# Three key heads computed in the recurrence's prologue, and a new order for the attention's first tiles

## The chip, the cores and the metric

The kernel runs on one core of a Trainium2 chip. The metric is the device time of one execution in microseconds (us), taken as the median of the runs. The core has five engines, each with a queue of its own that it works off in order: TensorE (PE in the profile, PEld for its weight loads), VectorE (DVE), ScalarE (ACT), GpSimd (POOL) and SyncE (SP), which here issues most of the DMAs.

## What is computed

The reference is a network of four parts with residual connections, on x of 4 batches x 512 rows x 512 columns and a context ctx of 4 x 512 x 256:

```python
x = x + _L0_xattn_ref(ctx_1024, _layernorm(x), ...)   # a state-space recurrence over the rows
x = x + _L0_ffn_ref(_layernorm(x), ...)               # 64 experts, 8 for each row
x = x + _L1_xattn_ref(_layernorm(x), ctx_1024, ...)   # attention, 16 heads of 128
x = x + _L1_ffn_ref(_layernorm(x), w1, w2)            # feed-forward, quantized weights and inputs
```

Two of them matter here. The recurrence, for each of 512 channels (four blocks of 128, c) and 16 states n, walks over the 512 rows:

```python
state = state * exp(delta * A) + (delta * u) * B      # delta, u, B, C come from projections of ctx
y = sum over n of state * C                           # then + D * u, times silu of the normed x
```

The attention's keys depend on ctx alone, and not on x:

```python
k = (ctx @ Wk).reshape(B, Skv, H, D)
k = k * rsqrt(mean(k * k, axis=-1) + 1e-5) * gk
```

So the 64 key heads (4 batches x 16) can be computed at any time before the attention reads them.

## The kernel before

The kernel is one program in four stages, each of which writes down the order of its instructions by hand: every call in the source puts its instructions at the end of its engines' queues, in the order of the calls.

**The recurrence** (`ssm_phase`) runs over `seq`, 128 steps q = (batch b, channel block c, pair of states i), 32 steps to a batch. A step needs three things. `inputs(q)` (L494) multiplies `du` by the rows of B, on POOL, into `dBu` (128x1024). `decays(q)` (L505) makes exp(delta * A) on ACT into `dA`. `scan(q)` runs a scan on DVE (L519) and multiplies by the rows of C (L520), on POOL where i is 0, 2 or 4 and on DVE otherwise. TensorE turns and sums the results (`sums`, L525). Beside this the steps carry work for the next batch (`ahead`), the values of the attention (`values`, L476, one PSUM bank with the tag pv, and `take_values`, L482, on ACT), and keys.

Ahead of the loop stands a prologue for batch 0: projections (`conv_0`), a convolution, `project`, `dt` (L420), then on ACT `steps_a` and `steps_ln`, on DVE `steps_b` (L445 to L447), which ends with delta, on POOL `step_du` (L455, and L458, which writes a reset into delta's first column after it was read), on ACT `decays(0)` and `decays(1)`, on POOL `inputs(0)` and `inputs(1)`. `rows(b, g)` (L413) loads four rows of B (`bb`) and four of C (`cb`), 1 MB each, spread over all partitions; for batch 0 the first group is queued after `take_project`, then `load_wv(0)` (L469) and the other three groups. At q = 0 ACT gets `silu_gz(0)` (L393), with a table load before and after it; at q = 1 TensorE gets a transposition of its result and then the first `values`; at q = 2 ACT gets `take_values` ahead of `decays(3)`.

**A key head** (`Keys`) is four calls. `task` (L1216) multiplies the context by the head's part of Wk, two blocks of 128 deep, into a PSUM bank `pk`. `evict` squares it (L1225) and scales it (L1226) on ACT, and stores kT by a DMA on SP (L1227). `squares` (L1236) sums the squares by eight small matmuls with a column of ones into `kpss`. `take` (L1248) copies the mean squares on ACT and stores them (L1250). `row` and `psum` say where the two rows and two banks are taken from.

Of the 64 heads, 15 stand in batches 0 to 2 of the recurrence (for the next batch), 16 in its last batch (those of batch 0, one every second step, `plan_key` from `last_q` on, their weights loaded four heads at a time by `key_at(..., keys.load, ...)` into two buffers with the tag dA), 17 in the routing stage, and 16, listed in `KEYS_LATE`, at the start of the attention.

**Routing and experts** follow. In the experts' stage the mean squares of all heads but the late ones are turned into factors (`key_norms`) and stored as rows.

**The attention** (`attend`) begins with the four row tiles of batch 0, i = 0 to 3. Their order is made from a list of `later(time, call)`, sorted by time; the times are only an order. Eight late keys come first (`some_keys`). Then 32 gathers of experts' results on POOL (`fetch`, L1874), each followed by an addition on DVE (`add`, L1882); after every eighth a tile is complete, gets its statistics (`stats`, L1888 on DVE and L1892, L1894 on POOL) and is normed (`normed`, xn_c, L1900). Tile i starts at `at = FRONT + i * WINDOW`: `turn_x` (L1907) turns the tile, `queries` for head groups 0 and 1 (L1953), `norm_q` (L1956 on ACT, L1962 on DVE, then rq by L1964, L1965 on POOL), `scale_q` (qn, L1971 on DVE), `turn_q` (pqt, L1980), `scores` (psc, L1987, then mx on DVE L1990 and e on ACT L1993), `weights` (L1998, L1999), `turn` (pet, L2052). Two late keys stand in each tile: `key_task` and `key_ends` (`squares`, then `take`). `last_norms` and `last_keys` then make the late heads' factors. After the tiles a loop over heads and tiles does the rest; the last stage, the feed-forward part, is woven into it.

Of the kernel before, what the change touches and what calls it, by code (L numbers as in the profile page):

```python
# [17 lines left out]
F32 = mybir.dt.float32  # L18
# [7 lines left out]
ALU = mybir.AluOpType  # L26
# [4 lines left out]
P = 128  # L31
B, S, DM = 4, 512, 512
NT = B * S // P
NC = DM // P
# [24 lines left out]
H, HD = 16, 128  # L59
HG = 4  # L60

KEYS_LATE = [(b, h) for b in (2, 3) for h in range(8, H)]
DH = 2048
RESET = 1e30
MAGIC = 12582912.0
# [177 lines left out]
def ssm_phase(ctx, cm, x_all, w, kv, router_stats):  # L243
# [4 lines left out]
    tc, nc = cm.tc, cm.nc  # L248
# [4 lines left out]
    ps = ctx.enter_context(tc.tile_pool(name="a_ps", bufs=1, space=PSUM))  # L253
    py = ctx.enter_context(tc.tile_pool(name="a_py", bufs=1, space=PSUM))
    pda = ctx.enter_context(tc.tile_pool(name="a_pda", bufs=2, space=PSUM))
    KC = CTX // P
# [10 lines left out]
    def load_ctx(b, again=False):  # L267

        t = pool[2].tile([P, KC, S], F32, name="ctxb")
        nc.sync.dma_start(t, w["ctxT"][:, b * S:(b + 1) * S].rearrange("(k p) s -> p k s", p=P))  # L270
        if again:
            st[b]["ctx"] = t
            return
        st[b] = dict(ctx=t, u=[], gz=[], delta=[], du=[], bb=[], cb=[],
                     mv=small.tile([P, NC, 2], F32, name="mv"))
# [3 lines left out]
    load_ctx(0)  # L279
    load_x(0)  # L280
    load_ctx(1)
    vecs = {}
    for n, shape in (("conv_w", [P, NC, DC]), ("conv_b", [P, NC]), ("D", [P, NC])):
        t = vecs[n] = cp.tile(shape, F32, name=f"v_{n}")
# [104 lines left out]
    def silu_gz(b):  # L389
        s = st[b]  # L390
        for c in range(NC):
            gz = pool[4].tile([P, S], F32, name="gz")
            nc.scalar.activation(gz, x_all[:, b * NC + c, :], AF.Silu, bias=s["nmr"][:, c:c + 1],  # L393
                                 scale=s["rstd"][:, c:c + 1])
            s["gz"].append(gz)
        tables(nc)
# [12 lines left out]
    def rows(b, g):  # L409

        for name, row in (("bb", g * NG), ("cb", DS + g * NG)):
            t = pool[4].tile([P, NG, S], F32, name=name, tag=name)
            nc.sync.dma_start(  # L413
                t, bc_dram[b, row:row + NG, :].unsqueeze(0).to_broadcast([P, NG, S]))
            st[b][name].append(t)

    def dt(b, c):

        pdt = st[b]["pdt"] = ps.tile([P, S], F32, name="pdt", tag="pa")
        nc.tensor.matmul(pdt, dtT[:, c * P:(c + 1) * P], st[b]["xd"][0:DR + 1, :], start=True,  # L420
                         stop=True)

    def steps_a(b):

        s = st[b]
        pdt = s["pdt"]
        s["e"] = pool[1].tile([P, S], F32, name="e")
        s["relu"] = pool[2].tile([P, S], F32, name="delta")
        nc.scalar.activation(s["e"], pdt, AF.Abs)
        nc.scalar.activation(s["relu"], pdt, AF.Relu)  # L430
        nc.scalar.activation(s["e"], s["e"], AF.Exp, scale=-1.0)
# [8 lines left out]
    def steps_b(b):  # L440


        s = st[b]
        t, delta = s.pop("pdt"), s.pop("relu")
        nc.vector.scalar_tensor_tensor(t, t, 1.0, s["e"], ALU.subtract, ALU.subtract)  # L445
        nc.vector.tensor_tensor(t, s["ln"], t, ALU.subtract)
        nc.vector.tensor_tensor(delta, delta, t, ALU.add)  # L447
        s["delta"].append(delta)

    def step_du(b):  # L450
        s = st[b]
        c = len(s["du"])
        delta = s["delta"][c]
        du = pool[2].tile([P, S], F32, name="du")
        nc.gpsimd.tensor_tensor(du, delta, s["u"][c], ALU.mult)  # L455


        nc.gpsimd.memset(delta[:, 0:1], RESET)  # L458
        s["du"].append(du)


# [24 lines left out]
    seq = [(b, c, i) for b in range(B) for c in range(NC) for i in range(NP)]  # L486
    dBus, dAs, hcs, yTs = {}, {}, {}, {}

    def inputs(q):
        if q < len(seq):  # L490
            b, c, i = seq[q]
            j = i % 2 * 2
            dBus[q] = pool[3].tile([P, 2, S], F32, name="dBu")
            nc.gpsimd.tensor_tensor(dBus[q], st[b]["bb"][i // 2][:, j:j + 2, :],  # L494
                                    st[b]["du"][c].unsqueeze(1).to_broadcast([P, 2, S]), ALU.mult)

    def decays(q, early=False):

        if q < len(seq) and q not in dAs:
            b, c, i = seq[q]  # L500
            dAs[q] = (pool[2].tile([P, 2, S], F32, name="dA") if early else
                      pda.tile([P, 2, S], F32, name="dA"))
            for j in range(2):
                n = 2 * i + j
                nc.scalar.activation(dAs[q][:, j, :], st[b]["delta"][c], AF.Exp,  # L505
                                     scale=negA[:, c, n:n + 1])
# [108 lines left out]
    def plan_key(q, b, h, bank):  # L615
        key_at(q, True, key_task, b, h, bank)
        key_at(q + 2, False, keys.evict)
        key_at(q + 2, True, keys.squares)
        key_at(q + 3, False, keys.take)
# [3 lines left out]
            key_at(b * SL + s - 3, False, keys.load, j, j + 1, pool[2], "k_w")  # L623
            plan_key(b * SL + s, b + 1, j, bank)
    last_q = (B - 1) * SL
    for h in range(H):
        plan_key(last_q + 2 * h, 0, h, "pin")
    for h, q in ((0, last_q - 8), (HG, last_q + 6), (2 * HG, last_q + 8), (3 * HG, last_q + 16)):
        key_at(q, True, keys.load, h, h + HG, pool[2], "dA")

    def key_steps(q, ends):
# [18 lines left out]
        stats(0, c)  # L650
    norm(0)
    dt(0, 0)
    steps_a(0)
    steps_ln(0)
    steps_b(0)
    step_du(0)
    decays(0)
    decays(1)
    inputs(0)
    inputs(1)  # L660
    load_wv(0)
    for g in range(1, DS // NG):
        rows(0, g)
    for q, (b, c, i) in enumerate(seq):
        inputs(q + 2)

        ahead_of = b + 1 < B and q % 2 == 0 and q > 0
        if ahead_of:
            take_values(*last)
        decays(q + 1)  # L670
        key_steps(q, False)
        if b > 0 and q % SL == 1:
            rows(b, DS // NG - 1)
        if i == 2 and q > 2:
            result(*seq[q - 3][:2])
        scan(q)
        if i == 1:
            direct(b, c)
        if q == 0:
            silu_gz(0)  # L680
        if q % SL == 8 and b + 1 < B:
            load_x(b + 1)
        if i == 2:
            take_gate(b, c)

        to = seq[q // NP * NP + NP][0:2] if q + NP < len(seq) else None
        if to is not None:
            if i == 3:
                steps_a(to[0])
                steps_ln(to[0])  # L690
            if i == 5:
                step_du(to[0])
        if b + 1 < B:
            ahead(b + 1, q % SL)
        if i == 1:
            gate(b, c)
        if q % 8 == 2 and q + 8 < len(seq):
            load_wv(q // 2 + 4)
        if q % 2:
            values((b + 1) % B, q % SL // 2, wvs[q // 8])  # L700
        elif q > 0 and not ahead_of:
            take_values(*last)
        last = (b + 1) % B, q % SL // 2
        sums(q - 1)
        if to is not None:
            if i == 2:
                dt(*to)
            if i == 4:
                steps_b(to[0])
        if b + 1 < B:  # L710
            ahead_ends(b + 1, q % SL)
        key_steps(q, True)
# [1130 lines left out]
def attend(ctx, cm, x_all, w, kv, y_dram, wk, pos, tern, late, ctx_k, wk_k, out):  # L1843
# [422 lines left out]
    keys = Keys(cm, w, kv, small, key_row, key_bank,  # L2266
                lambda b: (ctx_k[b], 0), direct=ms)
    keys.wk = wk_k
    first = KEYS_LATE[0][1]

    steps = []

    def later(time, f, *a):
        steps.append((time, len(steps), f, a))

    START, GAP, FLIGHT = 3.0, 1.35, 6.0
    FRONT, WINDOW = 21.0, 14.5

    wide = [pool[1].tile([P, KB, S], F32, name="yg_first", tag="eT")]
    wide += [pool[2].tile([P, HG, DM], F32, name="yg_more", tag="Wo") for _ in range(2)]  # L2280
# [27 lines left out]
    for i in range(NC):  # L2308
        end = START + ((i + 1) * TOPK - 1) * GAP + FLIGHT
        later(end + 0.1, stats, i, "c")  # L2310
        later(end + 2.3, normed, i, "c")
        at = FRONT + i * WINDOW
        later(at, turn_x, i)
        later(at + 0.5, key_task)
        later(at + 2.2, queries, 0, 0, i)
        later(at + 5.6, key_ends)
        later(at + 6.4, norm_q, 0, 0)
        later(at + 6.5, queries, 0, 1, i)
        later(at + 8.5, scale_q, 0, 0)
        later(at + 10, turn_q, 0, 0, i)  # L2320
        later(at + 10.4, key_task)
        later(at + 10.8, norm_q, 0, 1)
        later(at + 12.1, scores, 0, i)
        later(at + 12.9, scale_q, 0, 1)
        later(at + 13, key_ends)
        later(at + 14, turn_q, 0, 1, i)
        if i < KB - 1:
            later(at + 14.7, weights, 0, i)
        if i < KB - 2:
            later(at + 15, turn, 0, i)  # L2330
# [9 lines left out]
    def last_keys():  # L2340
        pr = ptr.tile([n_ms, P], F32, name="pkr", tag="pt")
        nc.tensor.transpose(pr, ms, cm.ident)
        rows = pool[1].tile([n_ms, P], F32, name="k_rows", tag="xn_d")
        nc.scalar.copy(rows, pr)
        for b in (2, 3):
            at = (b * H + first) * KB
            nc.sync.dma_start(kv["r"][at:at + n_ms // 2, :],
                              rows[(b - 2) * n_ms // 2:(b - 1) * n_ms // 2, :])


    for *_, f, a in sorted(steps, key=lambda x: x[:2]):
# [192 lines left out]
```

## Time and profile before

| | us |
|---|---|
| median of 3 runs | 2475.75 (2473.74 to 2478.19) |
| the profiled execution | 2472.46 |
| its span, first to last instruction | 2470.7 |
| TensorE busy in the span | 2337.7 (95%) |
| DVE, ACT, POOL busy | 1595.2, 1386.1, 1344.1 |
| first scan of the recurrence starts | 34.57 |
| last dBu of the recurrence starts (POOL) | 503.58 |
| first late key of the attention starts (TensorE) | 1310.51 |
| last pqt of the first four tiles starts (TensorE) | 1404.86 |

The profile is of one execution. A line of the timeline gives the start and the duration in us, the engine, the source line, the operation, the output and inputs by their names, the shapes, the number of instructions merged into the line, and in brackets the engine's idle time before it with what ended it. The page's busy rows cut the span into 40 equal slices; a digit is the busy share in tenths. A line of the waits names who waited for whom, then the total in us, the number of waits and the longest. The granted TensorE clock is given as a share of full speed.

### The profile page before, as it was taken

Reading aid. Unit: us, or ns where it says so; the run is one execution under the profiler, and the core shown is the slowest. Engines: PE = TensorE matmul, PEld = TensorE weight load, DVE = VectorE, ACT = ScalarE, POOL = GpSimd, SP = SyncE. Lnnn points to the kernel's source line nnn. Section 1 sums busy time; section 2 is a strip of 40 time slices with the busy share of each in tenths; the row PEclk is TensorE's granted clock in tenths of the full one; section 3 lists DMA queues with packets and bytes.
Section 4 is the critical chain, followed back from the end, with each engine's and each line's share of the span. In section 5 each row is a group of like instructions: output and inputs, shape, how many; then the busy total and the mean of one; then the engine's idle time right before and its main releaser. Section 6 shows DMA issues by size and latency. Waiting matters only on the chain. (4 is left out here: it accounts for less than half of the span.)

```text
span 2470.7 us, 29274 instructions
## 1 busy us (share of the span) xinstructions
PE 2337.7 (95%) x8915; PEld 1275.5 (52%) x8915; DVE 1595.2 (65%) x2848; ACT 1386.1 (56%) x2599; POOL 1344.1 (54%) x1323
## 2 busy tenths in 40 slices
PE   6989998988899999999998999999999999999998
PEld 2555555655556666666674444444444444444443
DVE  6999998966343444444324577667776777666655
ACT  6777777755333333342323466666666767667654
POOL 7999999950344455444434356356544665333323
PEclk8999999998999999999998999999999999999999
DMA  5252626343677777989866568778866887666530
GB/s 212 90 210 95 219 85 232 112 151 119 194 233 227 229 243 236 314 308 336 302 210 211 163 179 217 163 181 187 207 159 149 200 202 173 138 156 147 136 75 24
DMA packets 454245, 458.69 MB, mean 186 GB/s; under 512 B 289239, under 2 KB 330279, under 8 KB 449984
## 3 DMA queue, kind: packets, MB, share of 16 engines
q1 hardware_dynamic: 410622, 299.80, 43.4%
q0 software_dynamic: 41408, 156.76, 19.8%
q8 instruction: 73, 1.20, 0.2%
q14 instruction: 92, 0.75, 0.1%
q10 hardware_dynamic: 2050, 0.18, 0.1%
HBM read 312.74 MB, written 79.82 MB: 159 GB/s over the span
## 5 line engine op out<-in xcount | busy, mean ns | idle before, releaser
L1336 PE MATMUL pg<-xT,wg 128*128 128x284 f32 (+12 forms) x1536 | 392.7, 399 | 2.0 <-ACT xT L1303 1.1
L1990 DVE TENSOR_REDUCE mx<-psc 128x1 f32<-128x512 f32 x256 | 176.1, 688 | 244.4 <-PE psc L1987 244.0
L2018 POOL COPY planes<-e 128x512 int16<-128x512 int16 x174 | 119.1, 684 | 392.3 <-DVE e L1999 230.7
L1336 PEld LDWEIGHTS pg<-xT,wg 128*128 128x128 f32 x1536 | 277.8, 191 | 91.6 <-issue 40.9
L494 POOL TENSOR_TENSOR dBu<-bb,du 128x1024 f32<-128x1024 f32 x128 | 304.3, 2398 | 2.7 <-DVE dA L519 1.8
L1993 ACT ACTIVATE e<-psc,mx 128x512 f32<-128x512 f32 x256 | 176.3, 688 | 149.6 <-DVE mx L1990 81.8
L1987 PE MATMUL psc<-kT,qT 128*128 128x512 f32 x512 | 260.0, 594 | 0.0
L2059 PE MATMUL po<-eT,v 128*128 128x512 f32 x512 | 236.8, 605 | 10.4 <-ACT eT L2053 8.6
L1257 POOL DMA_INDIRECT xg<-xn_dram,tok x168 | 177.5, 1056 | 116.5 <-PE pt L1300 51.4
L1953 PE MATMUL pq<-Wq,xnT 128*128 128x512 f32 x512 | 232.7, 597 | 4.3 <-ACT xnT L1909 3.9
L2068 PE MATMUL px<-Wo,oT 128*128 128x512 f32 x512 | 231.2, 595 | 0.4 <-DVE qn L1971 0.4
L505 ACT ACTIVATE dA<-delta,negA 128x512 f32<-128x512 f32 x256 | 176.5, 695 | 52.1 <-DVE hc L520 29.1
L519 DVE TENSOR_TENSOR_SCAN dA<-dA,dBu 128x1024 f32<-128x1024 f32 x80 | 185.4, 2318 | 14.6 <-ACT dA L505 4.9
L1257 POOL DMA_INDIRECT wd<-down,widx x64 | 63.1, 986 | 237.9 <-PE po L1370 222.3
L2059 PEld LDWEIGHTS po<-eT,v 128*128 128x128 f32 x512 | 92.0, 189 | 147.5 <-issue 91.8
L1381 ACT COPY yo<-po 128x512 f32<-128x512 f32 (+3 forms) x64 | 37.5, 586 | 224.7 <-PE po L1370 185.3
L1953 PEld LDWEIGHTS pq<-Wq,xnT 128*128 128x128 f32 x512 | 96.5, 191 | 129.7 <-issue 110.4
L525 PEld LDWEIGHTS yT<-ident,hc 128*128 128x128 f32 x1024 | 119.5, 144 | 77.3 <-issue 40.5
L2068 PEld LDWEIGHTS px<-Wo,oT 128*128 128x128 f32 x512 | 95.1, 190 | 123.3 <-issue 102.8
L1874 POOL DMA_INDIRECT yg<-y_dram,pos x108 | 119.8, 1109 | 62.7 <-issue 50.4
L525 PE MATMUL yT<-ident,hc 128*128 128x128 f32 x1024 | 133.2, 278 | 19.8 <-DVE yg L559 9.2
L1381 DVE COPY yo<-po 128x512 f32<-128x512 f32 x68 | 46.9, 691 | 159.4 <-PE po L1370 159.4
(378 smaller groups left out, 4686.2 us busy)
## 6 DMA issues: line engine op xcount, KB each, us to landing
y_dram<-yo SPq DMA_DIRECT2D x110, 256.0 KB
bb<-bc_dram SPq DMA_DIRECT2D x16, 1024.0 KB
cb<-bc_dram SPq DMA_DIRECT2D x16, 1024.0 KB
v_dram<-v SPq DMA_DIRECT2D x64, 256.0 KB
k_dram<-k_kT SPq DMA_DIRECT2D x64, 256.0 KB
kT<-k_dram SPq DMA_DIRECT2D x64, 256.0 KB
rk<-r_dram SPq DMA_DIRECT2D x64, 256.0 KB
v<-v_dram SPq DMA_DIRECT2D x64, 256.0 KB
```

The source lines that it names most:

```text
L494: nc.gpsimd.tensor_tensor(dBus[q], st[b]["bb"][i // 2][:, j:j + 2, :], st[b]["du"][c].unsqueeze(1).to_broadcast([P, 2, S]), ALU.mult)
L505: nc.scalar.activation(dAs[q][:, j, :], st[b]["delta"][c], AF.Exp, scale=negA[:, c, n:n + 1])
L519: nc.vector.tensor_tensor_scan(*flat, 0.0, ALU.mult, ALU.add)
L525: nc.tensor.matmul(yT[:, lc, :], t[:, lc * P:(lc + 1) * P], cm.ident, is_transpose=True, start=first and lc == 0, stop=last, skip_group_ch ...
L1257: nc.gpsimd.indirect_dma_start(out=t[0:n, :], out_offset=None, in_=table, in_offset=bass.IndirectOffsetOnAxis(ap=index, axis=0))
L1336: nc.tensor.matmul(pg[:, 0:n], s["wg"][:, c, m * P:(m + 1) * P], s["xT"][:, c, 0:n], start=c == 0, stop=c == NC - 1)
L1953: nc.tensor.matmul(pq.rearrange("p h d -> p (h d)"), xnTs[b * NC + i][:, c, :], s["Wq"][:, c, :], start=c == 0, stop=c == NC - 1)
L1987: nc.tensor.matmul(pscore, st[b, g]["qT"][:, h, i * P:(i + 1) * P], ks[n], start=True, stop=True)
L1990: nc.vector.tensor_reduce(mx, pscore, AX.X, ALU.max, negate=True)
L1993: nc.scalar.activation(e, pscore, AF.Exp, bias=mx, accum_out=tot)
L2059: nc.tensor.matmul(po, v[:, kc, :], eT[:, kc, :], start=kc == 0, stop=kc == KB - 1)
L2068: nc.tensor.matmul(px, oTs[j * HG + h][:, i * P:(i + 1) * P], st[b, g]["Wo"][:, h, :], start=h == 0, stop=h == HG - 1)
```

## The change

Three heads of batch 0 (h = 0 to 2) move into the prologue. Their weights get a DMA of their own on SP, after the first loads, in a buffer of the tag Wv. Their two rows are parts of `x_all` that are not loaded yet (row tiles 15 down to 10), their banks are pin, yT and pin for `pk`, and pv for all three `kpss`. Two tasks are queued on TensorE after `dt`; the evictions and takes are queued on ACT after `steps_ln` and between the decays; the last take after `silu_gz(0)`. `load_wv(0)` and the row loads are called earlier, in the same order among themselves.

`step_du(0)` and `inputs(0)` of the first step go from POOL to DVE.

In the last batch of the recurrence the 16 places for keys are kept. The 13 other heads of batch 0 come first, then heads 13 to 15 of batch 3, which were late ones; the weight loads for heads 4 on come 6 steps earlier. `KEYS_LATE` shrinks from 16 to 13: in the attention's first tiles, tile 0 keeps two keys, and tiles 1 to 3 have one each. `WINDOW` goes from 14.5 to 12.0, which also puts the next tile's `turn_x` and first `key_task` ahead of `scores` and of the second `turn_q`; and the second `key_ends` goes from 13 to 12.2.

```diff
+EARLY = 3
-KEYS_LATE = [(b, h) for b in (2, 3) for h in range(8, H)]
+KEYS_LATE = [(b, h) for b in (2, 3) for h in range(8, H - EARLY * (b == 3))]
...
     load_ctx(1)
+    wk_first = pool[2].tile([P, KC, EARLY * HD], F32, name="k_w", tag="Wv",
+                            padded_shape=[P, KC, HG * HD])
+    nc.sync.dma_start(wk_first, w["Wk"][:, 0:EARLY * HD].rearrange("(k p) e -> p k e", p=P))
...
-    def step_du(b):
+    def step_du(b, by=nc.gpsimd):
...
-        nc.gpsimd.tensor_tensor(du, delta, s["u"][c], ALU.mult)
-        nc.gpsimd.memset(delta[:, 0:1], RESET)
+        by.tensor_tensor(du, delta, s["u"][c], ALU.mult)
+        by.memset(delta[:, 0:1], RESET)
...
-    def inputs(q):
+    def inputs(q, by=nc.gpsimd):
...
-            nc.gpsimd.tensor_tensor(dBus[q], st[b]["bb"][i // 2][:, j:j + 2, :],
+            by.tensor_tensor(dBus[q], st[b]["bb"][i // 2][:, j:j + 2, :],
...
-    for h in range(H):
-        plan_key(last_q + 2 * h, 0, h, "pin")
-    for h, q in ((0, last_q - 8), (HG, last_q + 6), (2 * HG, last_q + 8), (3 * HG, last_q + 16)):
+    ends = [(0, h) for h in range(EARLY, H)] + [(B - 1, h) for h in range(H - EARLY, H)]
+    for i, (b, h) in enumerate(ends):
+        plan_key(last_q + 2 * i, b, h, "pin")
+    for h, q in ((0, last_q - 8), (HG, last_q), (2 * HG, last_q + 2), (3 * HG, last_q + 10)):
...
     dt(0, 0)
+    firsts = []
+    for h in range(EARLY):
+        at = iter((NT - 2 * h - 2, NT - 2 * h - 1))
+        k = Keys(cm, w, kv, cm.k_small, lambda n, at=at: x_all[:, next(at), :],
+                 lambda shape, name, h=h: (py if name == "pk" and h == 1 else ps).tile(
+                     shape, F32, name=name,
+                     tag="pv" if name == "kpss" else "yT" if h == 1 else "pin"),
+                 lambda b: (st[b]["ctx"], 0))
+        k.wk[h] = wk_first[:, :, h * HD:(h + 1) * HD]
+        firsts.append(k)
+    for h in range(2):
+        firsts[h].task(0, h)
     steps_a(0)
     steps_ln(0)
-    steps_b(0)
-    step_du(0)
-    decays(0)
-    decays(1)
-    inputs(0)
-    inputs(1)
     load_wv(0)
     for g in range(1, DS // NG):
         rows(0, g)
+    firsts[0].evict()
+    firsts[0].squares()
+    firsts[2].task(0, 2)
+    firsts[1].evict()
+    firsts[0].take()
+    firsts[1].squares()
+    steps_b(0)
+    step_du(0, nc.vector)
+    decays(0)
+    firsts[2].evict()
+    firsts[1].take()
+    firsts[2].squares()
+    decays(1)
+    inputs(0, nc.vector)
+    inputs(1)
...
             silu_gz(0)
+            firsts[-1].take()
...
-    FRONT, WINDOW = 21.0, 14.5
+    FRONT, WINDOW = 21.0, 12.0
...
-        later(at + 10.4, key_task)
+        if i < NC - EARLY:
+            later(at + 10.4, key_task)
...
-        later(at + 13, key_ends)
+        later(at + 12.2, key_ends)
```

In `last_keys` the store of the late heads' factors is cut by the new lengths of the list (8 heads of batch 2, 5 of batch 3).

More of the change, by code (lines that the diff above doesn't have):

```diff
@@ L2268, in attend @@
     keys.wk = wk_k
-    first = KEYS_LATE[0][1]
     steps = []
@@ L2345, in last_keys @@
         for b in (2, 3):
-            at = (b * H + first) * KB
-            nc.sync.dma_start(kv["r"][at:at + n_ms // 2, :],
-                              rows[(b - 2) * n_ms // 2:(b - 1) * n_ms // 2, :])
+            at = [i for i, (c, _) in enumerate(KEYS_LATE) if c == b]
+            to = (b * H + KEYS_LATE[at[0]][1]) * KB
+            nc.sync.dma_start(kv["r"][to:to + len(at) * KB, :],
+                              rows[at[0] * KB:(at[-1] + 1) * KB, :])
     for *_, f, a in sorted(steps, key=lambda x: x[:2]):
```

## The prediction

> **What bounds the kernel now.** I read the busy lines of the page first, then the timeline of the prologue and of the attention's first tiles (the two places the diff touches), then the waits between them.
>
> ```profile
> DVE  6999998966343444444324577667776777666655
> POOL 7999999950344455444434356356544665333323
> ```
>
> Each slice is 61.8 us. In slices 0 to 7, the recurrence, POOL is full and DVE nearly so. POOL's waits between 37 and 510 us, the recurrence proper, are few:
>
> ```profile
> POOL hc L520 <- DVE hc L519: 9.0, 5, 2.2
> POOL dBu L494 <- DVE dA L519: 1.8, 3, 0.8
> POOL dBu L494 <- DMA bb<-bc_dram: 0.4, 1, 0.4
> POOL dBu L494 <- issue: 0.3, 1, 0.3
> ```
>
> So POOL idles 11.5 us in 473: the recurrence ends when POOL ends. Now how it starts (timeline, start and duration in us):
>
> ```profile
> 23.90 1.59 PE L420 MATMUL pdt<-xd,dtT 17*128 17x512 f32 x2 [0.92 <-ACT xd L406]
> ...
> 30.82 1.26 POOL L455 TENSOR_TENSOR du<-delta,u 128x512 f32<-128x512 f32 x1 [4.35 <-DVE delta L447]
> ...
> 32.27 2.75 ACT L505 ACTIVATE dA<-delta,negA 128x512 f32<-128x512 f32 x4 [3.79 <-POOL delta L458]
> 34.57 2.29 DVE L519 TENSOR_TENSOR_SCAN hc<-dA,dBu 128x1024 f32<-128x1024 f32 x1 [3.90 <-POOL dBu L494]
> ...
> 37.28 2.36 POOL L494 TENSOR_TENSOR dBu<-bb,du 128x1024 f32<-128x1024 f32 x1 [0.44 <-DMA bb<-bc_dram]
> ...
> 38.12 3.56 PE L476 MATMUL pv<-Wv,ctxb 128*128 128x512 f32 x4
> ```
>
> The reader is to see three things. POOL's third dBu starts at 37.28 because a row load landed then, not because POOL was late. ACT has a gap of 3.79 us before 32.27, PE one from 25.49 to 37.25. The clock is at half (0.50 in the windows from 24.4 to 41.5): four pv matmuls take 3.56 us there, and 1.88 later.
>
> The attention's first tiles (TensorE's timeline):
>
> ```profile
> 1355.99 1.12 PE L1980 MATMUL pqt<-ident,qn 128*128 128x128 f32 x4 [2.79 <-DVE qn L1971]
> ...
> 1374.03 0.66 PE L1980 MATMUL pqt<-ident,qn 128*128 128x128 f32 x4 [1.50 <-DVE qn L1971]
> ...
> 1385.77 1.88 PE L1216 MATMUL pk<-k_ctx,k_w 128*128 128x512 f32 x4
> ...
> 1404.86 0.66 PE L1980 MATMUL pqt<-ident,qn 128*128 128x128 f32 x4 [0.50 <-DVE qn L1971]
> ```
>
> The last two tiles are TensorE's (15.2 of 16 us, 14.5 of 15 busy); the chain that ended last runs through pk, kpss, pq there. Tiles 0 and 1 also wait for qn, behind POOL's gathers.
>
> **The change, the attention.** Three keys leave: per key pk 1.72 and kpss 0.79 us on the chain, 7.5 in all. The order also changes: with a window of 12.0, turn_x and the key task of the next tile stand ahead of scores and of the second turn_q (time 12.0 and 12.5 against 14), so TensorE has work while qn is made. I walked the new order with the durations of the rows.
> - Tile 0: qn is ready at 1355.94 as before, but xn_c of tile 1 was ready at 1351.35, so turn_x (0.44), scores (0.87), kpss (0.79) and the next pk (1.72) fill the 2.79 us hole. queries(0,0,1) start at about 1356.5, before 1360.59: 4.1 saved.
> - Tile 1: queries twice (3.43, 3.54), pet, kpss, pqt end near 1365.1. turn_x(2) needs xn_c, which before ended at 1366.07 and by POOL's new order (two gathers fewer ahead of rq) ends near 1366.2. The second qn needs rq, now behind gathers 28 to 30: they end near 1369.5, rq 1.3 and qn 0.7 bring 1371.7. TensorE idles 2.4 us. queries(0,0,2) start at 1372.2, before 1377.58: 5.4 saved.
> - Tile 2: 12.3 us from there (before 14.96), as no wait is left; tile 3 to its last pqt 11.2 (before 12.32), with 2.1 of wait for qn, since nothing stands beside that chain: sum 5.4 + 2.7 + 1.1 = 9.2.
> - The clock: an idle of 2.79 us was followed by half clock (pqt 1.12 for 0.66), one of 1.50 was not. Mine, 2.4, is nearer to 2.79: four matmuls of pq take 0.85 for 0.43, 1.7 lost.
>
> I take 9.2 - 1.7 = **7.5 saved**. Ends: 9.2 (clock stays up); 3.9 if only the tiles after the last gather gain (27.28 us from 1377.58 to 1404.86 against 23.4 by the walk). Past 1404.86 TensorE's order is unchanged, and the 40 us there (34.85 busy) start earlier: load_q(2), load_o and load_kv(3) are queued on SP behind fewer key stores.
>
> The Trainium skill, "TensorE: Matmul & The Clock Gate", Part 1, says that the gate watches a free-running window of some 3.4 us, and that one idle window halves the clock. By that rule taken alone 2.4 us of idling costs nothing and the sum here would be 9.2; the row at 1355.99 shows the clock lost after less.
>
> **The change, the prologue.** Removed from POOL: du 1.26, memset 0.10, first dBu 2.33. On DVE they take 0.69 (L447's row of this size), 0.06 and 1.22 (L520's row); at most POOL's own durations. DVE frees du at 31.4, before 32.2. But POOL then waits for bb until 37.28, and the load order on SP is unchanged. **POOL gains nothing from it**: at best the 0.44 us of the DMA wait, if rows land earlier, for which I see no reason.
>
> Added: wk_first, 384 KB on SP after 7.4 us; at the 289 GB/s of 5 to 10 us it needs 1.4 us, lands near 14, and is wanted at 25.3. Stores of k and ms go to SP behind the row loads, so they delay only the v stores (v is wanted again 12 us later). Squares and kT lie in rows of x_all that are loaded for batches 2 and 3, 40 steps later at the earliest, long after those stores: nothing.
>
> On TensorE, task 0 follows pdt at 25.3 at 0.85 a matmul; conv_0's burst from 6.77 sped up after 3.9 us and the one from 37.25 after 4.3, so this one, from 23.9, should near 27.8. Then pk0 ends at 28.45, pk1 at 30.2, pk2 at 32.7, with kpss between. On ACT the evictions (0.6 + 0.69, about 1.2 in a row) and takes (0.17) stand between ln, which ends at 28.49, and the decays: evict 28.5 to 29.7, 30.2 to 31.4, take, decays(0) 31.6 to 33.0, evict and take to 34.4, decays(1) to 35.8. Before: 35.04. So 3.0 of 3.9 us are hidden in ACT's gap. The first scan is 1.5 earlier, the second no earlier.
>
> Next is the added wait: the last take comes after silu_gz (5.5 us), and kpss holds the bank that pv needs. pv therefore cannot start before 41.5 (before 38.12), and at half clock ends at 45.05; v's copy stands ahead of decays(3) on ACT:
>
> ```profile
> 43.01 1.41 ACT L505 ACTIVATE dA<-delta,negA 128x512 f32<-128x512 f32 x2
> ...
> 44.51 2.30 DVE L519 TENSOR_TENSOR_SCAN dA<-dA,dBu 128x1024 f32<-128x1024 f32 x1
> ...
> 66.47 2.35 POOL L520 TENSOR_TENSOR hc<-hc,cb 128x1024 f32<-128x1024 f32 x1
> ```
>
> v copied at 45.65, decays to 47.05, fourth scan at 47.1: 2.6 late. DVE has next to no gap until the scan whose result POOL takes at 66.47; that ended at 65.55, 0.9 before. **POOL is 1.7 us late** from there, and keeps it. Ends: 0 (pv at full clock gives 0.9 late, which the 0.9 covers) and 6.2 (half clock through all three keys: take 4.5 later, fourth scan 7.1 late, less 0.9). The later keys of the recurrence keep their number and places; their weights are loaded 6 steps earlier, as the first buffer is free after one key. Nothing.
>
> The GPSIMD Engine Reference of the Trainium skill, section 1, says VectorE's operations with two SBUF inputs contend with GpSimd: against DVE doing dBu beside POOL. POOL's hc at 46.54 took 2.37 beside DVE's hc at 46.90 (1.22), the usual durations: I see no price; by the rule at most the 1.22 us would be lost, in a stretch where POOL waits anyway.
>
> **Sum.** -7.5 + 1.7 = -5.8. The profiled execution took 2472.46 (span 2470.70 and 1.76 around it), which gives 2466.7; the runs' median is 2475.75, 3.29 above it (2473.74 to 2478.19), so **2470.0**.
>
> **Rivals.**
> - B, the prologue costs nothing (pv fast, or the lateness lost in DVE's idle times, 2.2 twice behind POOL's x_all): -7.5 to -9.2, 2466.6 to 2468.3.
> - C, gathers set the first tiles, and only 3.9 is gained: -3.9 + 1.7, 2473.5.
> - D, slower. ACT is in order, and both decays stand behind evictions. If every key runs serially at half clock (one key: pk 3.42, kpss 1.6, eviction 1.2, take 0.17, together 6.4; 19.2 for three) less the 6.8 us from 25.5 to 32.27, 12.4 is lost: +4.9, 2480.7; with C's gain 2484. It decides once pk0 ends later than some 31, as when wk_first lands late. Against it: DMA is idle from 12.3 to 23.9.
> - E, it does not do what it says: DVE's inputs free POOL for a load that has not landed, and what the attention gains is given back by DVE's chain after 1405 (26.9 of 40 us busy, mx to e to eT): 2474 to 2477.
>
> **How the numbers follow.** 0.2% is 4.95 us, about what a measurement of this kernel can tell from no change: the bound is 2470.8. Forecast 0.46 (2467 to 2473; 0.31 under the bound), B 0.24 (faster), C 0.16 and E 0.05 (within), D 0.09 (slower). Faster 0.55, same 0.36, slower 0.09. The range, 2464.5 to 2477.0, takes B with 2 us for the spread of the medians, C and E; D stays out.
>
> **What would show it.** Right: dBu at 37.3 still behind DMA bb; pv's start at 41 to 42 behind the take; hc's wait for DVE near 66 to 68; POOL's last dBu (503.58 before) 1 to 3 us later; from attention's first pk (1310.51) to the last pqt 94.35 us before, 86.9 after. Wrong: POOL's third dBu well before 37; decays waiting for pk; TensorE idle over 3 us in tiles 1 to 3.

## The result, and the profile after

| | before | after |
|---|---|---|
| median of 22 runs each, us | 2478.40 | 2483.90 |
| ratio after / before | | 1.0021 [1.0011, 1.0031] |
| profiled execution (span), us | 2472.46 (2470.7) | 2480.31 (2478.6) |
| third scan of the recurrence starts | 42.09 | 52.68 |
| last dBu of the recurrence starts (POOL) | 503.58 | 516.12 |
| first pk to last pqt of the attention's first tiles | 94.35 | 88.66 |

The change makes the kernel slower: 0.21% of 2478.4 is 5.2 us (2.7 to 7.7). Nothing like the -5.8 of the prediction. The busy rows of the page after:

```profile
DVE  4999998975343444444323577667776778666655
POOL 5999999961343455444434456346544665333323
```

Slice 0 falls from 6 and 7 to 4 and 5, and slice 8, in which the recurrence ends, rises for POOL from 5 to 6. Both engines lost time in the first 62 us, and POOL ends later by it. The waits there, from 30 to 70 us (total, number, longest):

```profile
DVE hc L523 <- ACT dA L509: 14.8, 2, 14.4
...
PE pv L480 <- ACT k_ms L1275: 13.4, 1, 13.4
ACT k_ms L1275 <- DMA ms_dram<-k_ms: 11.0, 1, 11.0
POOL hc L524 <- DVE xin L327: 8.7, 1, 8.7
...
POOL dBu L498 <- DMA bb<-bc_dram: 3.1, 1, 3.1
```

Read it from the third line: a `take` on ACT (k_ms) waits 11.0 us for a DMA *out of* k_ms. Every other wait shown but the last hangs on it. ACT works in order, so the decays behind the take (dA) are late, so DVE's scan, so POOL's hc; and pv, whose bank the take must first empty. The timeline in order of time (start, duration):

```profile
29.65 0.20 ACT L1275 ACTIVATE k_ms<-kpss 128x4 f32<-128x4 f32 x1
...
30.66 3.39 POOL L498 TENSOR_TENSOR dBu<-bb,du 128x1024 f32<-128x1024 f32 x1 [4.54 <-DVE du L459]
...
32.18 2.29 DVE L523 TENSOR_TENSOR_SCAN hc<-dA,dBu 128x1024 f32<-128x1024 f32 x1 [0.34 <-ACT dA L509]
...
37.15 0.32 SPq L1277 DMA_DIRECT2D ms_dram<-k_ms  x1
37.16 2.35 POOL L498 TENSOR_TENSOR dBu<-bb,du 128x1024 f32<-128x1024 f32 x1 [3.12 <-DMA bb<-bc_dram]
...
51.10 0.17 ACT L1275 ACTIVATE k_ms<-kpss 128x4 f32<-128x4 f32 x1 [10.95 <-DMA ms_dram<-k_ms]
...
51.33 3.42 PE L480 MATMUL pv<-Wv,ctxb 128*128 128x512 f32 x4 [13.43 <-ACT k_ms L1275]
...
52.68 2.29 DVE L523 TENSOR_TENSOR_SCAN hc<-dA,dBu 128x1024 f32<-128x1024 f32 x1 [14.41 <-ACT dA L509]
```

The first take, at 29.65, fills one of the two buffers that `cm.k_small` has for k_ms, and the second take the other. The third needs the first buffer again, which is free once the first take's store of 2 KB has landed. SP issues that store only at 37.15, and it stands in SP's queue behind what is left of the 8 MB of row loads and the 0.5 MB of Wv issued from 25.16 on (from 37 to 51 us 5.70 MB were moved in all). SP's own waits put the late issue, too, down to the landing of those loads: its stores of kT and k_ms wait 2.1 us at a time for bb or cb. What the DMA engines did while ACT, DVE and TensorE stood still, and just after (columns: window, its length, busy time and instructions of PE, PEld, DVE, ACT, POOL, then granted clock, DMA share, GB/s):

```profile
41.00:51.00 10.00, 0.00 (x0) 0.00 (x0) 0.00 (x0) 0.00 (x0) 5.40 (x3) 0.50 0.98 399
51.00:56.00 5.00, 4.67 (x14) 2.58 (x15) 2.30 (x2) 3.27 (x7) 0.95 (x1) 0.67 0.04 5
```

The take is released at 51.10, when the big loads have come to an end. For ten microseconds three engines execute nothing. Compared with before, hc by hc, POOL's second hc (55.05) is 8.5 us late, the fourth 11.0, and all that follow are 10.7 to 12.8 late: its last dBu starts at 516.12, 12.5 later than before. The attention's first tiles give back some six (lines of TensorE: the start of the stretch measured below, and its end, 53.71 us later; before it took 59.62):

```profile
1355.44 3.68 PE L1980 MATMUL pq<-Wq,xnT 128*128 128x512 f32 x8
...
1409.15 0.92 PE L2007 MATMUL pqt<-ident,qn 128*128 128x128 f32 x4 [1.68 <-DVE qn L1998]
```

### The profile page after: what moved, and what is told of

Read it like the earlier page. It is cut to its first block, busy times and chain, and to the rows that moved or that the text cites. A ratio compares the mean times of both kernels' runs of the same rounds, so it can differ in the third digit from the quotient of the medians.

```text
span 2478.6 us, 29293 instructions
## 1 busy us (share of the span) xinstructions
PE 2336.6 (94%) x8915; PEld 1274.0 (51%) x8915; DVE 1599.3 (65%) x2851; ACT 1384.8 (56%) x2599; POOL 1340.4 (54%) x1320
## 5 line engine op out<-in xcount | busy, mean ns | idle before, releaser
L529 PEld LDWEIGHTS yT<-ident,hc 128*128 128x128 f32 x1024 | 119.1, 144 | 76.8 <-issue 41.5
```

Of the source, the lines that this page charges most:

```text
L529: nc.tensor.matmul(yT[:, lc, :], t[:, lc * P:(lc + 1) * P], cm.ident, is_transpose=True, start=first and lc == 0, stop=last, skip_group_ch ...
```

## The experiments

Every kernel was timed over five rounds against the kernel before on the same chip; ratios have their 95% interval. "The tiles" below is one stretch of TensorE's timeline: from tile 0's second run of eight pq to the start of the last pqt of the four tiles. It begins behind the load of Wq, for which TensorE waits by chance (0 us in the profile of before, 3.65 in a second one). Where it waited long, the eight pq that open the stretch are slower as well (5.40 to 6.59 us in place of 3.68, in six of the fourteen profiles), so that these stretches hold up to 2.9 us of that chance.

### Theory and rival: the buffer, or the work as such

**third_buffer**: the three first keys get a pool of their own with three k_ms buffers; nothing else differs from the changed kernel.

```diff
+    own = ctx.enter_context(tc.tile_pool(name="a_own", bufs=3))
     for h in range(EARLY):
-        k = Keys(cm, w, kv, cm.k_small, lambda n, at=at: x_all[:, next(at), :],
+        k = Keys(cm, w, kv, own, lambda n, at=at: x_all[:, next(at), :],
```

> The changed kernel, with a pool of three k_ms buffers for the prologue's keys in place of the shared pool of two. Theory (the third take waits 11.0 us on ACT for the first mean-square store, which lies behind 8 MB of row loads on SP's queue): that wait goes, the third take comes near 40.2 us, the third scan near 42 in place of 52.7, POOL's last dBu near 505 in place of 516, and the time is 9 to 11 us below the changed kernel, 4 to 6 below before. Rival (the keys' own work on TensorE and ACT is what costs): time within 2 us of the changed kernel.

Measured: ratio 0.9968 [0.9954, 0.9982], now faster than before, by 7.9 us (4.5 to 11.4). The wait is gone (the place of POOL's last dBu, 508.37, is 3 later than expected), and what follows it lies where it would without:

```profile
41.47 0.17 ACT L1276 ACTIVATE k_ms<-kpss 128x4 f32<-128x4 f32 x1
...
41.69 3.78 PE L480 MATMUL pv<-Wv,ctxb 128*128 128x512 f32 x4 [2.49 <-ACT k_ms L1276]
...
45.51 0.59 ACT L486 COPY v<-pv 128x512 f32<-128x512 f32 x1 [1.92 <-PE pv L480]
45.99 1.42 ACT L509 ACTIVATE dA<-delta,negA 128x512 f32<-128x512 f32 x2
...
47.50 2.30 DVE L523 TENSOR_TENSOR_SCAN dA<-dA,dBu 128x1024 f32<-128x1024 f32 x1 [2.15 <-POOL dBu L498]
...
68.34 2.35 POOL L524 TENSOR_TENSOR hc<-hc,cb 128x1024 f32<-128x1024 f32 x1 [1.17 <-DVE hc L523]
```

The scan at 47.50 starts 0.09 after the two decays ahead of it end (45.99 and 1.42); the profile names POOL's dBu instead, but this scan's own, the first of two from 42.41 on (4.66 for both), was done before 45.

The buffer is the cause of the loss: a third one alone brings the ratio from 1.0021 to 0.9968.

**other_queue**: two buffers as in the changed kernel, but the first keys' stores of k_ms are issued by ACT.

```diff
+        self.queue = self.nc.sync
...
-            self.nc.sync.dma_start(self.kv["ms"][:, i * self.KB:(i + 1) * self.KB], ms)
+            self.queue.dma_start(self.kv["ms"][:, i * self.KB:(i + 1) * self.KB], ms)
...
+        k.queue = nc.scalar
         firsts.append(k)
```

> The changed kernel with its two k_ms buffers, but the three mean-square stores of the prologue's keys are issued on ACT's queue in place of SP's. Theory (a store of 2 KB lands late because it is queued behind the row loads on SP's queue): ACT issues each in some 0.45 us, it lands a few us later, the third take is no longer held, and the time is within 2 us of third_buffer, 10 below the changed kernel. Rival (the 16 DMA engines are full, so any store lands only when the rows are in, near 50 us): as the changed kernel, within 2 us.

Measured: 0.9968 [0.9952, 0.9984], as with a third buffer. The third take starts at 42.42 and waits for no DMA (first store and third take):

```profile
32.03 0.37 ACTq L1279 DMA_DIRECT2D ms_dram<-k_ms  x1
...
42.42 0.17 ACT L1277 ACTIVATE k_ms<-kpss 128x4 f32<-128x4 f32 x1
```

What moved from 36 to 42.4 us (queue: packets, MB, share of 16 engines; q1 is SP's, q10 ACT's):

```profile
q1 hardware_dynamic: 372, 2.65, 98.2%
q10 hardware_dynamic: 288, 0.00, 2.5%
```

All three small stores together are 432 packets, so 288 are the first two: they went through while q1 was still busy with the rows. So it is the place in SP's queue that held the buffer, not the load on the DMA engines. How much of that is the late issue (ACT issues at 32.03, SP at 37.15) and how much the loads ahead in the queue, this run does not separate. The Trainium skill, "DMA: Bandwidth & Descriptors", section "Queues, rings and completion order", has the rule behind it: SP and ACT each own a row of rings on the same 16 engines, each ring is consumed in order, and an engine takes turns between the rows packet by packet. The two rows above agree.

### One half at a time

**prologue_alone**: the prologue as changed (two buffers), the attention and the late keys as before. Heads 0 to 2 are thus computed twice.

```diff
-KEYS_LATE = [(b, h) for b in (2, 3) for h in range(8, H - EARLY * (b == 3))]
+KEYS_LATE = [(b, h) for b in (2, 3) for h in range(8, H)]
...
-    FRONT, WINDOW = 21.0, 12.0
+    FRONT, WINDOW = 21.0, 14.5
...
```

> The prologue and DVE's first inputs as in the changed kernel; the attention, its 16 late keys and the recurrence's last batch as before (three heads are computed twice). Theory: recurrence 12 us longer as in the changed kernel, total 9 to 12 above before (the experts gave back 2.5 in the changed kernel's profile). Rival (the loss comes from the attention's new order or from the later stages): within 2 us of before.

**attention_alone**: the old prologue with the new attention. Heads 0 to 2 of batch 0 are not computed in it.

```diff
-KEYS_LATE = [(b, h) for b in (2, 3) for h in range(8, H)]
+KEYS_LATE = [(b, h) for b in (2, 3) for h in range(8, H - EARLY * (b == 3))]
...
-    FRONT, WINDOW = 21.0, 14.5
+    FRONT, WINDOW = 21.0, 12.0
...
```

> The prologue as before; the recurrence's last batch and the attention's first tiles as in the changed kernel. The keys of heads 0 to 2 of batch 0 are not computed: other data is stored in their place, so that the loads stay. Theory: recurrence as before, last dBu of POOL near 503.6; first pk to last pqt 88 to 89 us in place of 94.4; total 4 to 6 us below before. My blind walk said 7.5. Rival (the new order gains nothing beyond the noise): within 2 us of before.

Measured: prologue alone 1.0048 [1.0031, 1.0065], which is +11.9 us (7.7 to 16.1), with POOL's last dBu 12.3 later (515.84). Attention alone 0.9977 [0.9960, 0.9994], -5.7 us (-9.9 to -1.5). 0.48% less 0.23% is 0.25%, and the whole change measured 0.21%: within their intervals the two halves add up. One expectation for attention_alone did not come: from the first pk to the last pqt it takes 92.1 us and not 88 to 89, with 7.25 us of waiting for Wq in them.

### What is left of the prologue's cost

**take_early**: third_buffer, and the last take stands ahead of `silu_gz`.

```diff
     decays(1)
+    firsts[2].take()
...
             silu_gz(0)
-            firsts[-1].take()
```

> As third_buffer, with the last take put ahead of silu_gz, after decays(1). Theory of the blind prediction (the take behind silu_gz holds pv, v and so the fourth scan: POOL 1.7 us late): 1 to 2 us below third_buffer, pv's start at about 37.5 in place of 40.5. Rival (POOL's place is set by the bb load alone, and DVE's lateness is absorbed): within 0.5 us of third_buffer.

Measured: 0.9970 [0.9956, 0.9984]; the times don't tell it from third_buffer, but intervals as wide as these would not show 1 to 2 us either. The take now ends at 37.22, but pv starts at 40.31 and not then: on TensorE it stands behind the transposition of gz, which waits for `silu_gz` (until 39.40). In the profiles pv is thus 1.4 us earlier than in third_buffer, and POOL's last dBu 1.8 (506.61 and 508.37), one profile each.

**inputs_on_pool**: third_buffer, with `step_du(0)` and `inputs(0)` back on POOL.

```diff
-    step_du(0, nc.vector)
+    step_du(0)
...
-    inputs(0, nc.vector)
+    inputs(0)
```

> third_buffer with step_du(0) and inputs(0) back on POOL. Theory of the blind prediction (POOL waits for the second bb load in any case, so DVE's part buys nothing): within 1 us of third_buffer, POOL's third dBu still near 37.3 us. Rival (it buys POOL its 3.7 us): 3 to 4 us above third_buffer.

Measured: 0.9972 [0.9954, 0.9989]; not told apart from 0.9968, though the rival's 3 us lie within these intervals. POOL's third dBu there:

```profile
38.23 2.36 POOL L498 TENSOR_TENSOR dBu<-bb,du 128x1024 f32<-128x1024 f32 x1 [1.01 <-DMA bb<-bc_dram]
```

POOL does the extra work (du, memset, dBu) and still arrives 1.01 us before the row load has landed. At this place DVE's first inputs buy nothing. Whether they buy something later is not shown: POOL's last dBu is 1.9 us later here (510.31 and 508.37), in one profile each, and the two profiles already differ by 0.5 us when pdt starts.

**rows_first**: third_buffer, and the second load of `bb` is queued ahead of the first `cb` and of Wv, so that POOL does not wait for it.

```diff
-    rows(0, 0)
+    rows(0, 0, ("bb",))
+    rows(0, 1, ("bb",))
+    rows(0, 0, ("cb",))
...
-        rows(0, g)
+        rows(0, g, ("cb",) if g == 1 else ("bb", "cb"))
```

> third_buffer with the second bb load moved ahead of the first cb load and of Wv on SP's queue. Theory (with DVE's first inputs POOL is free from 34.8 and waits 3.0 us for that load): the load lands some 3.8 us earlier, POOL's third dBu starts near 34.8, and the time falls by 2 to 3 us. Rival (the lateness returns at the next load or at DVE's scans, as POOL's waits for DVE grow): within 1 us of third_buffer.

Measured: 0.9984 [0.9969, 1.0000], no gain over third_buffer. POOL does its second and third dBu in one run from 31.61, but waits 0.94 for the next `bb` at 42.87 and 1.17 for DVE at 68.21, where third_buffer stood at 68.34. The wait that was removed came back later, for the most part as waiting for DVE's scans; the last dBu starts at 507.98, 0.4 earlier than in third_buffer.

### Keys or order

**old_order**: third_buffer with the old window, so three keys fewer in the attention, in the old order.

```diff
-    FRONT, WINDOW = 21.0, 12.0
+    FRONT, WINDOW = 21.0, 14.5
...
-        later(at + 12.2, key_ends)
+        later(at + 13, key_ends)
```

> third_buffer with the attention's window at 14.5 and the second key_ends at 13 as before, still with 13 late keys. Theory (the three keys give about half, the new order the rest): 2 to 4 us above third_buffer. Rival (the order gives nothing, since the gathers' DMAs hold the tiles): within 1 us of third_buffer.

**order_alone**: the kernel before with the opposite edit alone (12.0 and 12.2); all 16 late keys stay, nothing is in the prologue. **third_again**: third_buffer once more, beside it.

> The kernel before with one thing changed: the window of 12.0 and the second key_ends at 12.2, all 16 late keys still there and nothing in the prologue. Theory: it is the new order that shortens the first tiles, and the keys were filler that stood beside the chain through qn; then this kernel is 3 to 8 us below the kernel before (ratio 0.997 to 0.999), and from the first pk to the last pqt it takes 86 to 92 us against 94.35. Rival: the order pays only where the keys leave, since without that each tile has two keys to fit in and TensorE is full; then it is within 2 us of the kernel before, and those 94 us stay.

> The same kernel as third_buffer, beside order_alone on one chip. If the moved keys have a worth of their own on top of the order, it is below order_alone by 2 us or more (by its earlier ratio 0.997 of the kernel before); if the order is all, order_alone is as fast or faster, since it has no work in the prologue, where third_buffer's POOL was 4.8 us late.

**order_again** is order_alone once more, and **before_again** the kernel before against itself.

> The same kernel as order_alone (window 12.0 with all 16 late keys), for a second profile and a second ratio. In the first profile TensorE waited 3.98 us for the load of Wq in tile 0, and its 8 pq took 6.52 us; the 95.8 us from the first pk to the last pqt hold this. If that was chance and the order itself shortens the tiles, this profile shows 87 to 92 us, and the ratio is again 0.996 to 0.999. If the order gains nothing while the keys stay, the stretch is 94 us or more again, without such a wait, and the ratio is 0.999 to 1.001.

> The kernel before, unchanged, timed against itself and profiled a second time: how far one profile and one ratio can be trusted. The ratio should have 1 in its interval; if it is off by 0.1% or more, differences of that size between experiments mean nothing. Its stretch from the first pk to the last pqt should be 94 us again within 1 us if the old order is what sets it, and 90 to 100 if the landing of loads and gathers does.

| kernel | late keys | order | ratio | the tiles, us |
|---|---|---|---|---|
| before, before_again | 16 | old | 0.9998 [0.9981, 1.0016] | 59.6, 60.9 |
| prologue_alone | 16 | old | 1.0048 [1.0031, 1.0065] | 60.8 |
| old_order | 13 | old | 1.0010 [0.9995, 1.0024] | 61.3 |
| order_alone, order_again | 16 | new | 0.9977 [0.9961, 0.9994], 0.9977 [0.9962, 0.9993] | 59.1, 58.0 |
| after | 13 | new | 1.0021 [1.0011, 1.0031] | 53.7 |
| third_buffer, third_again | 13 | new | 0.9968 [0.9954, 0.9982], 0.9969 [0.9951, 0.9987] | 54.9, 56.2 |
| the other five with both | 13 | new | | 54.4, 52.9, 54.5, 53.4, 53.3 |

In the tiles, taking the keys away shows no gain (61.3, one profile, against a mean of 60.4), the order alone 1.9 (mean 58.55), and both together 6.2 (mean of eight 54.2). In time, the new order with 13 late keys is worth more than expected: old_order lies 0.42% above third_buffer, some 10 us in place of 2 to 4. Why the keys alone gain nothing is seen in the pqt of old_order, the tiles 0 to 3:

```profile
1369.70 1.12 PE L2008 MATMUL pqt<-ident,qn 128*128 128x128 f32 x4 [2.78 <-DVE qn L1999]
...
1389.28 1.04 PE L2008 MATMUL pqt<-ident,qn 128*128 128x128 f32 x4 [3.25 <-DVE qn L1999]
...
1405.73 0.63 PE L2008 MATMUL pqt<-ident,qn 128*128 128x128 f32 x4 [1.47 <-DVE qn L1999]
...
1420.24 1.08 PE L2008 MATMUL pqt<-ident,qn 128*128 128x128 f32 x4 [1.68 <-DVE qn L1999]
```

Where before waits 2.79, 1.50, 0.50 and 0.50 for qn, TensorE now waits 2.78, 3.25, 1.47 and 1.68. The keys that left had stood beside the chain pq, sq, rq, qn; without them TensorE waits for it, 3.9 us more in all. It waits for qT ahead of psc as well (0.72 in tiles 2 and 3), and works longer at half clock: the pk behind the wait of 2.78 takes 3.52, before 2.05. With the new order the next tile's turn_x and scores stand there. Of the expectation for order_alone the time came (-5.7 us both times) and its place did not: from the first pk to the last pqt there are 95.8 and 93.5 us, with 3.98 and 1.84 us of waiting for Wq in them, and 59.1 and 58.0 in the tiles, with eight pq of 6.52 and 5.40 us in place of 3.68 behind that wait. So by the tiles the rival is right and the order pays fully only if keys leave, but up to some 2 us of the difference may be the chance of that wait. The times do not show it: attention_alone, with 13 late keys, has the same 0.9977 as order_alone with 16. Whether the keys' leaving adds to the order is open.

Something is open on the other side too. In third_buffer POOL ends 4.8 later and the tiles gain 4.9 (mean of 54.9 and 56.2, from 60.4): a sum near zero, but -7.9 us (-11.4 to -4.5) and -7.7 (-12.2 to -3.2) were measured. The profiles are not typical of the runs: third_buffer's took 2483.87 us, the longest of its 12, 12.2 above their median and 11.4 above the profiled execution of before; third_again's, 2482.11, is the longest of 12 too. So they cannot place the rest. Routing alone, from the end of POOL's last dBu to the first pg of the experts, takes 133.6 to 143.1 us in the fourteen profiles, in no order that follows the edits.

The fastest kernels found are third_buffer, other_queue, take_early and inputs_on_pool, not told apart, 0.3% below the kernel before and 0.5% below the changed one. Order_alone gets 0.23% with two numbers changed; beside third_again, on one chip, the difference is 0.0008 with overlapping intervals, and so not resolved.

## Why the prediction was wrong, step by step

**The step that failed** is the added wait. The prediction put it as "the last take comes after silu_gz (5.5 us), and kpss holds the bank that pv needs. pv therefore cannot start before 41.5", and of the stores, "Stores of k and ms go to SP behind the row loads, so they delay only the v stores". The first sentence saw the bank that the take must empty and ACT's order ahead of it, but not the buffer that the take must fill. The second saw the queue and the backlog, and asked only who stands behind these stores in the queue. It did not ask who waits for a buffer that they read. Those sentences give +1.7 us for the recurrence. In the trace pv started at 51.33 and POOL's last dBu was 12.5 late. None of the three signs of being wrong that the prediction names came up: POOL's third dBu stayed at 37.16, no decay waited for pk, and TensorE idled at most 1.66 us at a time for qn in the tiles 1 and 2 and 1.68 in tile 3.

With the buffer mended, the working of that step is seen to be nearly exact up to the point that it covers: pv at 41.69 (41.5 in the prediction), the fourth scan at 47.50 (47.1), hc at 68.34 (66.47 + 1.7 = 68.2), behind a wait for DVE, as it said.

**"and keeps it"** was wrong as well, by less. Set against before, hc by hc, third_buffer's POOL is 1.9 late there, 3.7 three hc later, 6.7 at most and 4.8 at the end; other_queue ends 2.4 late, take_early 3.0, and before_again 1.0 without any edit. The waits of the later steps are not fixed; a small shift moves them.

**"POOL gains nothing from it"** was right at the place that it speaks of. The third dBu started at 37.16 (37.28 before), now behind 3.12 us of waiting for `bb`, and inputs_on_pool shows it behind the same load.

**ACT's evictions** are hidden, and in the changed kernel's profile better than worked out. The first scan was expected 1.5 earlier and the second no earlier; they were 2.4 and 2.2 earlier (32.18 and 34.71, before 34.57 and 36.87). The prediction let task 0 run at half clock; in this profile the granted clock is 1.00 in the windows from 22 to 33 us:

```profile
24.60 3.70 PE L1243 MATMUL pk<-ctxb,k_w 128*128 128x512 f32 x8
```

That is luck. In third_buffer, with the same instructions up to here, pk follows pdt without a gap too, but the granted clock is 0.50 from 26 to 28, the eight pk take 5.40, and the scans start at 33.33 and 36.01, 1.2 and 0.9 earlier than before, near the working; in take_early they take 6.43, and the first scan (34.55) gains nothing. The rival D needed half clock through all three keys: the third task took 1.96 in every profile, so it did not occur, and the kernel was about as slow as D said (2480.7) for another reason.

**The attention's -7.5** was about right in size: 88.66 instead of the 86.9 from first pk to last pqt, and 6.2 saved in the tiles. Attention_alone has -5.7 for it. Its first clause, "Three keys leave: per key pk 1.72 and kpss 0.79 us on the chain, 7.5 in all", is not borne out: without the new order the keys' leaving shows no gain (old_order). The walk through the new order is what held, since it put both edits together: it had TensorE wait 2.4 us in tile 1 and 2.1 in tile 3, and the changed kernel waits 1.66 and 0.98, and 0.73 and 1.68.

**The clock in the tiles.** The prediction took 1.7 us off for a wait of 2.4. In third_again:

```profile
1382.74 0.63 PE L2008 MATMUL pqt<-ident,qn 128*128 128x128 f32 x4 [2.73 <-DVE qn L1999]
1383.21 5.30 PE L1981 MATMUL pq<-Wq,xnT 128*128 128x512 f32 x8
```

The eight pq take 5.30 where the changed kernel's at that place took 3.60: 1.7 lost, though not at once. The pqt still took 0.63, and the granted clock is 1.00 until 1383 and 0.50 from 1384 to 1387. But in order_again a wait of 2.33 cost nothing (0.63 for the pqt, 1.88 for the pk after it, the clock 1.00 throughout). In the changed kernel one of 1.66 was followed by a granted clock of 0.50 from 1379 to 1382:

```profile
1378.36 1.85 PE L2014 MATMUL psc<-kT,qT 128*128 128x512 f32 x2
1380.00 2.90 PE L1243 MATMUL pk<-k_ctx,k_w 128*128 128x512 f32 x4
```

At full clock these take 1.02 and 1.88. The 1.85 lost is about the prediction's 1.7, by luck, as the wait was shorter than its 2.4. The length of one wait does not decide it, and the prediction's choice by the nearest length was too simple. The Trainium skill, "TensorE: Matmul & The Clock Gate", Part 1, says that the gate's window is free-running, and that the moment of a change depends on where in the window the first matmul lands: that waits of like length end differently agrees. That the clock falls after waits shorter than its window of some 3.4 us is not what it says, and these rows show it.

**GpSimd beside VectorE.** "I see no price" was wrong, and harmless. POOL's dBu at 30.66, beside DVE's of 1.22 us, took 3.39 instead of 2.35. The Trainium skill's "GPSIMD Engine Reference", section 1, speaks of contention there, and the row shows 1.04 us of it; in third_buffer it is 3.38 again. In inputs_on_pool, where DVE makes no dBu beside them, POOL's first two take 4.65 together, the usual time; but POOL's hc beside DVE's hc lost nothing either, as the prediction read, so what sets such pairs apart is not shown. The loss falls in the time in which POOL then waits for `bb`.

In sum, by the profiles: +12.5 from the prologue and -6.2 from the tiles make +6.3, and +5.2 (2.7 to 7.7) was measured. The prediction had +1.7 and -7.5. Nearly all of the error is one wait: without it, in third_buffer, -7.9 (-11.4 to -4.5) was measured, around the -5.8 of the prediction.

## What to carry to other kernels

For each instruction that is moved, list the buffers that it fills as well as those that it empties, count how often each is filled before its reader is done, and remember that a store is a reader: it holds its buffer until it has landed, and here it landed only when the loads issued ahead of it on its queue were through. A few kilobytes should not share a queue with megabytes that were issued just ahead, or should have buffers enough to wait. And work that leaves a stage saves its duration only where nothing waits beside it: before it is taken out, see what chain it covered, and put other work in its place.

## What the runs showed of the hardware that was not expected

- A store of 2 KB, issued by SP behind the rest of 8.5 MB of loads, landed only when the loads ended, some 13.9 us after its issue (37.15 to 51.10); from ACT's queue two such stores were moved beside the same loads, within 10.4 us of the first one's issue (32.03 to 42.4).
- Two operations with two inputs each, on POOL and DVE at once: POOL's dBu took 3.39 instead of 2.35 us beside DVE's dBu; POOL's hc at 46.54, beside DVE's hc, took the usual 2.37.
- TensorE's clock may be halved some time after a wait rather than with it: pqt 0.63, then eight pq in 5.30 instead of 3.60 (after 2.73 us of waiting), with the granted clock at 0.50 from 1.3 us after the wait's end on, and nothing of the kind after 2.33.
- The same instructions in the prologue met a full clock in some profiles (the first eight pk 3.70) and a halved one in others (5.15 to 6.43).
- The kernel before, against itself: 0.9998 [0.9981, 1.0016]. Yet two profiles of it differ by 3.2 us in the attention's first 94 us, and one of them holds 3.65 us of waiting for the load of Wq there, the other none.
